# Graph network on one core: SyncE fetches one chunk of edges in some units row by row

## The chip, the cores and the metric

The kernel runs on one core of one Trainium2 chip. The metric is the device time of a run in microseconds (us); of several runs the median is given. The profile is that of one execution, with its own time.

## The reference

Four graph layers follow each other on 12500 nodes of 128 features and 212500 edges, which are sorted by their destination. Each layer adds to `x`: `x = x + layer(relu(layernorm(x)))`. The first is a pair of graph attention convolutions, the second a transformer convolution with a feed-forward part, the third takes a maximum over messages, and the fourth a mean over neighbours. The last two are what this change touches; cut to what matters they are:

```python
# layer 3
msgs = z[dst] @ Wd + z[src] @ Ws + edge_weight[:, None] * ww[None, :] + bm
agg  = segment_max(msgs, dst)
x    = x + relu(z @ W1a + agg @ W1b + b1) @ W2 + b2
# layer 4
h      = relu(layernorm(x))
sums   = segment_sum(h[src], dst)
x      = x + sums / maximum(counts, 1)
```

Each pass over the edges reads one table row for each edge, `table[src[e]]`, and reduces the rows of equal `dst`.

## The kernel before

The nodes are cut into 98 tiles of 128 (T = 98), the edges into 1661 chunks of 128 edges, and the chunks into 98 units of 17 (U = 17). In a unit the chunks are taken in six groups, five of 3 and one of 2 (GS = 3, NG = 6). As edges are sorted by destination, tile t needs the chunks of unit t and a few of its neighbours: 23 windows.

There are five edge passes, one after the other: two for the attention convolutions (`gat`), one for the transformer convolution (`attn`), then the maximum's (`maximum`, table `ts_`, rows of 512 bytes) and the last sum's (`total`, table `th`, rows of 516 bytes). In each, line 1245 fetches the rows of a chunk: one indirect DMA of GpSimd (POOL) for 128 edges, whose row numbers stand in a column of `IDX`. So each pass has 1661 gathers. A group's rows land in a tile `g` of 3 chunks; the maximum's pass has 20 such buffers, the sum's 24.

What follows a gather in the maximum: PE adds the chunk's part of the weights (lines 1711 and 1713, into `pg`), DVE runs a scan over the edges (line 1716), PE transposes (line 1722), ACT copies (line 1726). In the sum nothing stands between the gather and the last matmul. In both, ACT makes or casts a one-hot matrix for each batch of up to four windows (`sef`, line 1291, in the sum from a stored `se`), and PE multiplies the one-hot matrix with the chunk's rows into the tile's sum `acc` (line 1300). A buffer `g` comes free when its last reader has finished.

A tile ends with `ends`: SP loads `gt` (line 1307), ACT copies `acc` (line 1321), and the pass's `post` follows. In the sum that is `after_sum`: DVE divides and adds `x` (line 942 makes `o`), and SP stores `o` to the output (line 944, `out_x` in the trace). SP (SyncE) also loads `x` of the next tile (line 737) and `se` (line 1262) or the features of its edges.

The order is written by hand. `edge_pass` puts generators on a calendar of rounds, 24 rounds for a unit (RU = 24), each with a rank within its round; in every round each live generator takes one step. The gathers of unit u start 24 rounds before the round u x 24, one group every four rounds; the batches of tile t lie in the rounds from t x 24 + 10 (sum) or + 12 (maximum) on. Each engine executes its instructions in the order in which they are written there. A DMA's wait holds up all that stands behind it on the engine that issues it.

Before the first pass, `prepared` sorts out the edge lists: it holds the source numbers of all edges in `sd` (128 partitions, 13 chunks each) and writes them, transposed, to `IDX`.

Of the kernel before, what the change touches and what calls it, by code (L numbers as in the profile page):

```python
# [65 lines left out]
def gnn_kernel(ctx, tc, a, out):  # L66
# [18 lines left out]
    ww_d = dram.tile([3, D], BF16, name="ww_d")  # L85
    feat_d = dram.tile([T, 5, EW], BF16, name="feat_d")
    last_d = dram.tile([T, 5, EW], BF16, name="last_d")
    ewf_d = dram.tile([3, CP * P], BF16, name="ewf_d")
    first_d = dram.tile([1, (CP + 16) * P], BF16, name="first_d")
    xd = dram.tile([NP, D], F32, name="xd")  # L90
# [197 lines left out]
    def chunks(out, x, on):  # L288

        o = out.rearrange("p (r b) -> p r b", b=RC)  # L290
        for b0 in range(0, RC, 4):
            n = min(4, RC - b0)
            px = psum([P, 4, P], "b", "px")
            for b in range(n):
                PE.transpose(px[:, b, :], x[:, (b0 + b) * P:(b0 + b + 1) * P], ident)
            yield
            on(o[:, :, b0:b0 + n].rearrange("p r b -> p b r"), px[:, :n, :])
# [118 lines left out]
    def prepared(wp):  # L416
        tn_i = wp.tile([P, 1], I32, name="tn_i")
        GP.iota(tn_i, pattern=[[0, 1]], base=0, channel_multiplier=P)
        tid = wp.tile([T, 1], I32, name="tid")
        GP.iota(tid, pattern=[[0, 1]], base=0, channel_multiplier=1)  # L420
        tn = wp.tile([P, 1], F32, name="tn")
        V.tensor_copy(tn, tn_i)
        tn1 = wp.tile([P, 1], F32, name="tn1")
        V.tensor_scalar_mul(tn1, tn, -1.0)
        tn2 = wp.tile([P, 1], F32, name="tn2")
        V.tensor_scalar_add(tn2, tn, float(P))
        yield

        w = rd_[:, 1:EW + 1]
        eq = wp.tile([T, EW - P], BF16, name="eq")
        long_ = wp.tile([T, 1], F32, name="long_")
        V.scalar_tensor_tensor(eq, w[:, P:], 0.0, w[:, :EW - P], op0=ALU.add, op1=ALU.is_equal,
                               accum_out=long_)
        yield
        f = wp.tile([T, 2], F32, name="f")
        V.tensor_scalar(f[:, 0:1], rd_[:, 0:1], tn[:T, :], long_, op0=ALU.is_ge, op1=ALU.max)
        V.tensor_scalar(f[:, 1:2], rd_[:, EW + 1:], tn2[:T, :], f[:, 0:1], op0=ALU.is_lt,  # L440
                        op1=ALU.max)
        V.tensor_scalar_min(f[:, 1:2], f[:, 1:2], 1.0)
        yield
        p2 = psum([P, P], "mm", "p2")
        PE.transpose(p2[:1, :T], f[:, 1:2], ident[:T, :T])
        yield
        flag = wp.tile([1, T], F32, name="flag")
        V.tensor_copy(flag, p2[:1, :T])
        zr = wp.tile([1, T], F32, name="zr")
        V.memset(zr, 0.0)  # L450
        ord_ = wp.tile([1, T], F32, name="ord_")
        V.tensor_tensor_scan(ord_, flag, zr, 0.0, op0=ALU.add, op1=ALU.add)
        V.tensor_copy(NOV, ord_[:, T - 1:T])

        at = wp.tile([1, T], F32, name="at")
        V.scalar_tensor_tensor(at, flag, -float(2 * T), ord_, op0=ALU.mult, op1=ALU.add)
        V.tensor_scalar_add(at, at, float(2 * T - 1))
        yield
        pfl = psum([P, P], "mm", "pfl")
        PE.matmul(pfl[:, :T], ones[0:1, :], flag, start=True, stop=True)  # L460
        p3 = psum([P, P], "mm", "p3")
        PE.transpose(p3[:T, 0:1], at, ident[0:1, 0:1])
        yield
        V.tensor_copy(FLAG, pfl[:, :T])
        at_i = wp.tile([T, 1], I32, name="at_i")
        V.tensor_copy(at_i, p3[:T, 0:1])
        GP.indirect_dma_start(out=list_d, in_=tid, in_offset=None,
                              out_offset=bass.IndirectOffsetOnAxis(ap=at_i[:, 0:1], axis=0),
                              bounds_check=T - 1, oob_is_err=False)
        SY.dma_start(LIST, list_d.rearrange("(p t) c -> p (t c)", p=1))  # L470
        yield

        yield from chunks(IDX, sd, V.tensor_copy)

        ch = wp.tile([P, RC * P], F32, name="ch")
        V.tensor_tensor(ch, dd[:, 1:], dd[:, :RC * P], ALU.not_equal)
        yield
        yield from chunks(FIRST, ch, S.copy)
        m = wp.tile([P, RC * P], BF16, name="m")
        S.mul(m, ch, -BIG)  # L480
        SY.dma_start(first_d[0, P:(CP + 1) * P].rearrange("(p f) -> p f", p=P), m)
        yield
        dl = w
        V.tensor_scalar(dl, w, tn1[:T, :], FAR, op0=ALU.add, op1=ALU.min)
        V.tensor_scalar_max(dl, dl, -1.0)
        yield
        xb = wp.tile([T, EW], BF16, name="xb")
        S.copy(xb, dl)
        SY.dma_start(feat_d[:, 2, :], xb)
        hi, lo = yield from square(wp, dl, [T, EW], "q")  # L490
        for k, y in ((3, hi), (4, lo)):
            SY.dma_start(feat_d[:, k, :], y)
        yield
# [707 lines left out]
    def zero_rows(pool):  # L1201
# [3 lines left out]
        for _ in zeroed(gen_d, z, 7):  # L1205
            for _ in range(2 * RU):
                yield

    class Pass:


# [10 lines left out]

        made, whole = True, True

        def __init__(self):
            self.rhs, self.gs, self.f, self.fa, self.x, self.n0 = {}, {}, {}, {}, {}, {}
            self.st, self.se, self.acc = {}, {}, {}

# [6 lines left out]
        def x_load(self, t):  # L1235
            if self.source is not None:
                self.x[t] = features(self.source, t, self.width)
            yield

        def gather(self, u, i):  # L1240
            c, n = groups_of(u)[i]
            g = self.pool.tile([P, GS, self.wid], self.dt, name="g", bufs=self.bufs)
            for j in range(n):
                k = u * U + c + j
                GP.indirect_dma_start(  # L1245
                    out=g[:, j, :], out_offset=None, in_=self.table,
                    in_offset=bass.IndirectOffsetOnAxis(ap=IDX[:, k:k + 1], axis=0))
            self.gs[u, i] = g
            yield
# [81 lines left out]
    def edge_pass(name, table, wid, dt, wids, work_of, post, extra=()):  # L1331
        nonlocal ps_now
        w = work_of
        with tc.tile_pool(name=name, bufs=2) as pool, \
                tc.tile_pool(name="ps_" + name, bufs=1, space=PSUM) as pp, tc.manual_schedule():
            ps_now, w.pool, w.table, w.wid, w.dt, w.wids = (pp, w.banks), pool, table, wid, dt, wids
            cal = {}

            def at(r, rank, g):
                cal.setdefault(r, []).append((rank, g))  # L1340

            for u in range(T):
                r0 = u * RU
                at(r0 - RU, 0, w.load(u))
                at(r0 + RU - 4 - w.tail[0] * (u == T - 1), 0, w.load2(u))
                for i, _ in enumerate(groups_of(u)):
                    at(r0 - RU + i * RG, 0, w.gather(u, i))
                    at(r0 + i * RG, 5, w.e1(u, i))
                    if w.e2_at is not None:
                        e2_at = w.e2_at if u < T - 2 else w.e2_last or w.e2_at  # L1350
                        at(r0 + e2_at[i] - w.tail[0] * (u == T - 1), 4, w.e2(u, i))
                if w.chain_at is not None:
                    at(r0 + w.chain_at - w.tail[0] * (u == T - 1), 3, w.chain(u))
                n = len(w.batches(u))
                rt = r0 + w.tile_at
                loads = rt - RU
                rt -= w.tail[1] * (u == T - 2) + w.tail[2] * (u == T - 1)
                at(min(loads, rt + RU - 9 - 3 * (n - 1) - 2), 0, w.tile_load(u))
                at(rt, 0, w.x_load(u))
                for b in range(n):  # L1360
                    at(rt + RU - 9 - 3 * (n - 1 - b), 2, w.batch(u, b, n))
                at(rt + RU - 4, 1, w.ends(u, post))
            for g in extra:
                at(0, 1, g(pool))
            live, r = [], min(cal)
            while live or cal:
                live += cal.pop(r, [])
                live.sort(key=lambda g: g[0])
                live = [g for g in live if next(g[1], live) is not live]
                r += 1  # L1370
# [116 lines left out]
        V.tensor_tensor(c, x, b, ALU.subtract)  # L1487

    class gat(Pass):
        chain_at, e2_at, tile_at = RU + 5, range(RU + 13, 2 * RU + 1, 2), 2 * RU  # L1490

        def __init__(self, c, source=None):
# [116 lines left out]
            return r  # L1609

    class attn(Pass):
        bufs, source, width = 17, x2d, 2 * D
        chain_at, tile_at = RU + 7, 2 * RU + 2
        e2_at = [RU + 15 + r for r in (0, 2, 4, 6, 7, 11)]
# [68 lines left out]
            return r  # L1683

    class maximum(Pass):
        feats, bufs, source, made = last_d, 20, xd, False
        tile_at, tail = 12, (0, 0, 8)
        banks = {"pm": 1, "x": 2, "acc": 1, "pg": 2, "mm": 2}
# [45 lines left out]
            return r  # L1734

    class total(maximum):
        bufs, made = 24, True
        tile_at, tail = 10, (0, 0, 0)
        banks = {"acc": 2, "mm": 2}
# [173 lines left out]
```

## Time and profile before

| | |
|---|---|
| median of 10 runs | 14941.93 us (14930.65 to 14956.68) |
| the profiled execution | 14932.26 us |
| its span | 14930.6 us |
| maximum's gathers, from and to | 9794 to 12395 us of the span |
| last sum's gathers, from and to | 12484 to 14901 us |
| a gather on POOL | 947 ns |
| POOL, PE, ACT, DVE busy | 53%, 52%, 31%, 31% of the span |

The page gives for each engine its busy time as a share of the span; what an engine waits for, and its register and semaphore instructions, are not counted as busy. The table of windows gives the same for stretches of the span, here the two passes that change. A line such as `L1245 POOL DMA_INDIRECT g<-th,IDX` names the code line, the engine, the operation and what is written from what. In timelines, the bracket behind an instruction says how long its engine sat idle ahead of it, and what ended that. "remote" stands for a releaser that the profile could not name, "issue" for time in which the engine waited for nothing that the profile shows.

### The profile page before, as it was taken

The page shows a single profiled execution, that of the slowest core. Times are in us where ns is not written, and L with a number is a line of the kernel's source. Part 1 is how long each engine was busy: PE and PEld are TensorE (multiplying, and loading weights), DVE is VectorE, ACT ScalarE, POOL GpSimd, SP SyncE. Part 2 cuts the span into 40 slices and gives each one's busy share as a digit, 9 for nine tenths or more (in the row PEclk, how much of TensorE's full clock was granted, in tenths as well). Part 3 has the DMA queues.
Part 4 walks back from the last instruction along what each step waited for, and adds up shares of the span by engine and source line. Part 5 has one row for each costly group of instructions (what it writes and reads, how often), then busy time and mean ns, then how long its engine had stood idle before and what let it go on. Part 6 is the DMA issues. An engine that isn't in the chain of part 4 may idle for free. (4 is left out here: it accounts for less than half of the span.)

```text
span 14930.6 us, 149840 instructions
## 1 busy us (share of the span) xinstructions
PE 7823.4 (52%) x47184; PEld 6072.7 (41%) x47185; DVE 4584.4 (31%) x15188; ACT 4646.7 (31%) x13171; POOL 7876.6 (53%) x8330
## 2 busy tenths in 40 slices
PE   4444444444555555455555555567888774333334
PEld 2222222223444444344444444445666553333333
DVE  4333333332333333344444444423333331000000
ACT  4444444442333333233333333323333332111111
POOL 3455455445555555444444444446555565666666
PEclk5555555555555655677777777777777776666666
DMA  4222122123333333333333333322222222222222
GB/s 112 54 55 49 48 49 49 48 53 81 86 86 86 85 83 86 91 100 97 96 98 101 97 96 98 101 60 79 73 75 75 76 76 59 67 71 68 68 67 69
DMA packets 759391, 1146.93 MB, mean 77 GB/s; under 512 B 224152, under 2 KB 491623, under 8 KB 758479
## 3 DMA queue, kind: packets, MB, share of 16 engines
q0 software_dynamic: 292368, 610.29, 17.3%
q1 hardware_dynamic: 465536, 526.83, 11.2%
q8 instruction: 374, 6.13, 0.2%
q14 instruction: 441, 3.61, 0.1%
q10 hardware_dynamic: 672, 0.07, 0.0%
HBM read 964.76 MB, written 171.69 MB: 76 GB/s over the span
## 5 line engine op out<-in xcount | busy, mean ns | idle before, releaser
L1245 POOL DMA_INDIRECT g<-t,IDX x3322 | 3147.3, 947 | 2940.4 <-issue 1951.4
L1300 PE MATMUL acc<-xf,sef 128*128 128x131 f32 (+2 forms) x13458 | 2743.8, 366 | 1088.0 <-issue 413.7
L1300 PEld LDWEIGHTS acc<-xf,sef 128*128 128x128 f32 x13458 | 2387.8, 263 | 1295.2 <-issue 514.1
L1245 POOL DMA_INDIRECT g<-tkv,IDX x1661 | 1574.5, 948 | 2000.5 <-DVE xf L1675 1483.9
L1245 POOL DMA_INDIRECT g<-ts__84,IDX x1661 | 1571.2, 946 | 1120.9 <-issue 417.7
L1245 POOL DMA_INDIRECT g<-th,IDX x1661 | 1571.7, 946 | 934.0 <-issue 539.2
L1300 PE MATMUL acc<-g,sef 128*128 128x129 f32 x4486 | 884.3, 376 | 1564.1 <-ACT sef L1291 1145.4
L1300 PEld LDWEIGHTS acc<-g,sef 128*128 128x128 f32 x4486 | 818.1, 282 | 1630.3 <-ACT sef L1291 1193.0
L1291 ACT CAST sef<-se 128x512 f32<-128x512 fp8e4 (+1 forms) x1755 | 1030.5, 599 | 1203.4 <-remote 915.1
L1528 PE MATMUL ex<-ADX,st 128*128 128x6 bf16 x4486 | 363.3, 176 | 1214.6 <-ACT st L1134 482.8
L1716 DVE TENSOR_TENSOR_SCAN fm<-n,fm,pg 128x384 f32<-128x384 bf16 (+1 forms) x585 | 567.0, 969 | 1346.1 <-PE pg L1713 602.1
L1315 DVE COPY_PREDICATED r<-FLAG,gt 128x129 f32<-128x129 int32 (+2 forms) x490 | 145.0, 296 | 2570.7 <-ACT r L1321 1792.6
L1528 PEld LDWEIGHTS <-st 128*128 128x128 fp8e4 x4486 | 334.1, 116 | 1434.1 <-issue 755.5
L1651 DVE TENSOR_TENSOR g<-qe,g 128x384 f32<-128x384 f32 x586 | 310.6, 530 | 1609.1 <-remote 1309.9
L1726 ACT COPY xf<-pt_f 128x384 f32<-128x384 f32 x586 | 270.6, 462 | 1270.0 <-PE pt_f L1722 384.1
L1141 PE MATMUL pm_st<-fe,NF 5*128 5x384 bf16 (+2 forms) x877 | 381.6, 458 | 532.2 <-ACT se L1134 430.0
L1646 PE MATMUL qe<-q,st 128*128 128x128 bf16 x6729 | 585.9, 249 | 57.9 <-issue 40.8
L1149 PE MATMUL pm_se<-NF,fa 5*128 5x128 bf16 x4486 | 614.1, 277 | 0.0
L1300 PEld LDWEIGHTS <-se 128*128 128x128 fp8e4 x2243 | 238.4, 130 | 912.3 <-issue 559.0
L1134 ACT ACTIVATE se<-pm_se,ones 128x512 fp8e4<-128x512 f32 (+1 forms) x585 | 391.4, 669 | 696.5 <-remote 458.8
L1300 PE MATMUL acc<-xs,se 128*128 128x201 bf16 x2243 | 483.6, 368 | 196.6 <-ACT se L1134 133.1
L1134 ACT ACTIVATE st<-pm_st,ones 128x384 fp8e4<-128x384 f32 (+2 forms) x877 | 469.6, 536 | 358.6 <-PE pm_st L1141 197.5
(1099 smaller groups left out, 12495.8 us busy)
## 6 DMA issues: line engine op xcount, KB each, us to landing
se<-se_d SPq DMA_DIRECT2D x294, 368.0 KB
st<-st_d SPq DMA_DIRECT2D x196, 368.0 KB
g<-t,IDX POOLq DMA_INDIRECT x3322
n<-first_d SPq DMA_DIRECT2D x97, 544.0 KB
st_d<-st SPq DMA_DIRECT2D x98, 368.0 KB
se_d<-se SPq DMA_DIRECT2D x98, 368.0 KB
g<-tkv,IDX POOLq DMA_INDIRECT x1661
g<-ts__84,IDX POOLq DMA_INDIRECT x1661
```

What stands on the lines that cost most here:

```text
L1134: S.activation(out, pm[:, :out.shape[1], :], AF.Relu, scale=-1.0, bias=ones[:, 0:1], saturate=False)
L1141: PE.matmul(pm[:, :n, :].rearrange("p j e -> p (j e)"), NF, f[:, c * P:(c + n) * P], start=True, stop=True)
L1149: PE.matmul(pm[:, j, :], f[:, (c + j) * P:(c + j + 1) * P], NF, start=True, stop=True)
L1245: GP.indirect_dma_start(out=g[:, j, :], out_offset=None, in_=self.table, in_offset=bass.IndirectOffsetOnAxis(ap=IDX[:, k:k + 1], axis=0))
L1291: S.copy(se, self.se[t][:, at, :])
L1300: PE.matmul(acc[:, :m], se[:, j, :], x[:, i, :], start=(b == 0 and j == 0), stop=(b == n - 1 and j == len(ws) - 1))
L1315: V.copy_predicated(r[:, :w], FLAG[:, t:t + 1].to_broadcast([P, w]), self.gt[:, :w])
L1528: PE.matmul(ex[:, 6 * k:6 * k + 6], st, ADX[:, t, :, :].rearrange("p s v -> p (s v)"), start=(first and c0 == 0), stop=(stop and c0 + n - ...
L1646: PE.matmul(qe[0][:, k - c0, :], st, self.q[t][:, s * D:(s + 1) * D], start=(first and s == 0), stop=(stop and s == 2))
L1651: V.tensor_mul(k, qe[0][:, :n, :], k)
L1716: V.tensor_tensor_scan(fm[:, :m, :].rearrange("p j e -> p (j e)"), self.n0[u][:, cols], pg, self.prev, op0=ALU.add, op1=ALU.max)
L1726: S.copy(ft[:, :m, :D], pt[:, :m, :])
```

## The change

In the preparation the source numbers are also written to a table in device memory, `src_x`, one 4-byte number for each edge. In the maximum's pass, in each sixth unit (u = 5, 11, ..., 95), and in the last sum's, in each fourth (u = 3, 7, ..., 95), POOL no longer gathers the unit's last chunk. SP loads that chunk's 128 source numbers into one partition (`rw`), reads them into registers, sixteen at a time, and starts one DMA for each row, from `table` at the register's row to partition q of a tile of its own, `gx` (two buffers). These rows are spread over 136 rounds in the maximum and 88 rounds in the sum, from 124 (maximum) or 76 (sum) rounds ahead of the unit's first round to 11 rounds behind it, with the load of `rw` four rounds earlier; in each round they come first (rank -1). The group's other chunk is gathered by POOL as before, into the same `gx`. The other three passes have `by_row = None`.

```diff
+    src_x = dram.tile([CP * P, 1], I32, name="src_x")
...
+        ch = wp.tile([P, RC * P], F32, name="ch")
+        V.tensor_copy(ch.bitcast(I32), sd)
+        SY.dma_start(flat(src_x), ch.bitcast(I32))
+        yield
         yield from chunks(IDX, sd, V.tensor_copy)
-        ch = wp.tile([P, RC * P], F32, name="ch")
...
+    RR = 16
+    row_regs = [SY.alloc_register(f"row{i}") for i in range(RR)]
...
+        def row_units(self):
+            if self.by_row is None:
+                return [], 0
+            span = self.by_row * RU - 4
+            return [(u, RU // 2 - span) for u in range(T - 1) if u % self.by_row == self.by_row - 1
+                    and u * RU + RU // 2 - span >= -RU], span
+
+        def fetch_rows(self, u, span):
+            g = self.gx[u] = self.pool.tile([P, 2, self.wid], self.dt, name="gx", bufs=2)
+            rw = self.pool.tile([1, P], I32, name="rw", bufs=2)
+            e0 = (u * U + U - 1) * P
+            SY.dma_start(rw, src_x[e0:e0 + P, :].rearrange("(o f) c -> o (f c)", o=1))
+            for r in range(4):
+                yield
+            q = 0
+            for r in range(span - 4):
+                while q < P and q * (span - 4) < (r + 1) * P:
+                    if q % RR == 0:
+                        SY.load(row_regs, rw[0:1, q:q + RR])
+                    v = SY.snap(row_regs[q % RR], min_val=0, max_val=NP - 1)
+                    SY.dma_start(g[q:q + 1, 1, :], self.table[ds(v, 1), :])
+                    q += 1
+                yield
+
         def gather(self, u, i):
             c, n = groups_of(u)[i]
-            g = self.pool.tile([P, GS, self.wid], self.dt, name="g", bufs=self.bufs)
+            by_row = i == NG - 1 and u in self.gx
+            if by_row:
+                g, n = self.gx.pop(u), n - 1
+            else:
+                g = self.pool.tile([P, GS, self.wid], self.dt, name="g", bufs=self.bufs)
...
+            units, span = w.row_units()
+            for u, r in units:
+                at(u * RU + r, -1, w.fetch_rows(u, span))
...
     class maximum(Pass):
+        by_row = 6
     class total(maximum):
+        by_row = 4
```

More of the change, by code (lines that the diff above doesn't have):

```diff
@@ L1223, in gnn_kernel @@
         made, whole = True, True
+        by_row = None
         def __init__(self):
+            self.gx = {}
             self.rhs, self.gs, self.f, self.fa, self.x, self.n0 = {}, {}, {}, {}, {}, {}
@@ L1489, in gnn_kernel @@
     class gat(Pass):
+        by_row = None
         chain_at, e2_at, tile_at = RU + 5, range(RU + 13, 2 * RU + 1, 2), 2 * RU
@@ L1611, in gnn_kernel @@
     class attn(Pass):
+        by_row = None
         bufs, source, width = 17, x2d, 2 * D
```

## The prediction

> **What bounds the kernel now.** I first read the page's busy shares. POOL is the busiest engine at 53%, next to PE at 52%, so no engine is full over the whole span. The table of windows then splits off the two passes that change.
>
> ```profile
> PE 7823.4 (52%) x47184; PEld 6072.7 (41%) x47185; DVE 4584.4 (31%) x15188; ACT 4646.7 (31%) x13171; POOL 7876.6 (53%) x8330
> core 0: us, PE busy (x) PEld busy (x) DVE busy (x) ACT busy (x) POOL busy (x), PEclk, DMA share, GB/s
> 9794.00:12395.00 2601.00, 2014.99 (x11184) 1511.98 (x11184) 789.69 (x2155) 809.45 (x1874) 1570.21 (x1660) 0.73 0.28 75
> 12484.00:14901.00 2417.00, 864.41 (x4342) 799.40 (x4342) 92.13 (x376) 336.00 (x660) 1570.40 (x1660) 0.60 0.28 68
> ```
>
> The maximum's gathers run for 2601 us and the last sum's for 2417 us, 1661 gathers in each: 26.5 and 24.7 us a unit, 1.566 and 1.455 us a gather. POOL is busy for 60 to 65% of these windows. DMA is at 28%, so bytes bound nothing.
>
> Next, the gather's line in the sum's window: what its engine sat idle for.
>
> ```profile
> L1245 POOL DMA_INDIRECT g<-th,IDX x1660: 942/947/1064, 12483.7 to 14899.8; - x185
>   issue: 538.9, 1480
>   PE acc L1300: 231.2, 66
>   remote: 159.0, 99
> ```
>
> A gather is 0.947 us, and "issue" is 0.30 us between two in a row, so back to back they come every 1.25 us: 21.25 us for a unit's 17. What lies over that pace (2417.3 - 1661 x 1.25 = 341 us, and 2600.9 - 2076 = 525 us in the maximum) is time in which POOL waited for a free gather buffer, which PE's last matmul releases. So POOL isn't late in either pass. In the maximum, the matmul that reads a chunk comes 80 to 92 us after its gather was issued, and that gather had landed after some 2.3 us.
>
> The timeline shows how the consumers lag in the sum.
>
> ```profile
> 12582.31 0.51 ACT L1291 CAST sef<-se 128x384 f32<-128x384 fp8e4 x1 [21.79 <-remote]
> 12603.85 0.94 POOL L1245 DMA_INDIRECT g<-th,IDX  x1 [0.30 <-issue]
> 12619.44 0.27 ACT L1321 COPY r<-acc 128x129 f32<-128x129 f32 x1 [36.62 <-remote]
> 12621.35 0.94 POOL L1245 DMA_INDIRECT g<-th,IDX  x1 [16.56 <-PE acc L1300]
> ```
>
> While gathers run back to back, from 12484 to 12605, ACT's casts wait 21 us and then 36 us for PE's releases, though PE's matmuls of one batch took 2 us. The releases come on steps of 0.70 us, up to 5.6 us apart. POOL runs out of buffers, stops for 16.56 us, and within that stop the releases speed up and the tile ends. So the sum is set by consumers, whose pace depends on whether POOL is gathering. After the last gather the sum's tiles take 6.8, 6.2 and 4.5 us (take 6), the maximum's 20.3, 20.0 and 17.9 (take 20).
>
> **The change, part by part.** It removes 16 gathers from the maximum (units 5 to 95, every sixth) and 24 from the sum (3 to 95, every fourth): 40 of 3322.
>
> Upper bound of the gain, POOL's own pace: at the passes' means 16 x 1.566 + 24 x 1.455 = 60 us. At the bare 1.25 us it is 50 us.
>
> Lower estimate, consumers' pace: let a tile take R us while POOL runs and Q while it stops. Sum: 21.25/R + 3.42/6 = 1, so R = 49 us. One gather less takes 1.25 us out of the running time, in which 1.25/49 of a tile was done, made up in 0.15 us of stop: gain 1.10 us, x24 = 26 us. Maximum: 21.25/R + 5.25/20 = 1, so R = 28.8; 1.25/28.8 x 20 = 0.87, gain 0.38 us, x16 = 6 us. Together 32 us. I take the middle of 32 and 60, near 45 us: the R-and-Q split treats a stop as quiet from its first moment, while the releases in the stop above were only fast after some 10 us, so the worth of a gather lies above 32 us. If nothing is gained, because the stops only lengthen, it is 0.
>
> What SP adds: 40 loads of 512 B, 320 register loads of 16 values each, and 5120 single-row DMAs, beside its 4100 DMAs of now. No row of before shows a one-row DMA with a register offset. The nearest are the preparation's one-partition DMAs.
>
> ```profile
> 31.27 0.21 SPq L403 DMA_DIRECT2D list_d<-none  x1
> 55.32 0.30 SPq L470 DMA_DIRECT2D LIST<-list_d  x1
> 13016.57 0.43 SPq L1307 DMA_DIRECT2D gt<-gen_d  x1
> 13028.26 0.70 SPq L1307 DMA_DIRECT2D gt<-gen_d  x1
> ```
>
> So 0.21 to 0.30 us for the issue. The register instructions (the trace has them, the page counts them as not busy) were 3 to 192 ns, and a load of one register 0.46 to 0.49 us in quiet stretches: for 16 values between 0.46 and 16 x 0.49 = 7.8 us, 0.03 to 0.49 us a row. Clean, a row is therefore 0.24 to 0.98 us; I take 0.40 (0.25 + 0.10 + 0.05), nearest to one-partition DMAs, with a load that costs about twice a single one.
>
> Room: four units of the sum are 98.7 us. SP's own 4 DMAs a unit are 1.6 us, 6.4 us in four, which leaves 92.3/128 = 0.72 us a row. In the maximum, six units are 159 us, less 17 us of SP's own DMAs: 1.1 us a row. At 0.40 both fit and the rows are hidden in SP's time of waiting; SP waits 1784 us for line 942 alone:
>
> ```profile
> SPq L944 <- DVE o L942: 1783.9, 70, 100.2
> ```
>
> That wait is also where the danger is. SP works in order. The rows of unit u are spread over the rounds from 76 before to 11 after its start, ahead of everything else in their round, so between two stores of `out_x` (line 944) stand 34 or 35 rows, and behind each store stand the next tile's x, se and gt. Those four DMAs were issued within 2 us of each other; now 35 rows x 0.40 = 14 us stand among them in by-row stretches. The se loads are a tile ahead and gt is used only at a tile's end, so I cost this at nothing while it stays under a tile's 24.7 us. If that cover is gone it costs what the rival below says. A row also waits for DVE's `o` two tiles back, since the store ahead of it does; the gather had four units of lead, the rows keep about two.
>
> A rule speaks against the whole idea. The Trainium skill ("DMA: Bandwidth & Descriptors", section "Bandwidth") holds that transfers under 64 KB are mostly overhead and should be batched. These rows are 512 B: one gather of 128 rows is 1.25 us of POOL, the same rows are 128 x 0.40 = 51 us of SP. The same page ("Latency and other measured facts") gives a register load a floor of about 600 ns; by it 8 loads cost 4.8 us a unit, as good as nothing here.
>
> The bytes are the same as before. The added table of sources (832 KB, one copy on DVE and one DMA in the preparation) I put at 0 to 3 us: the copy is bounded by DVE rows of some 2 us, and the preparation's end waits for other loads. The first three passes are unchanged.
>
> Sum for the likeliest case: 14932.3 - 45 + 1 = 14888 us for the profiled execution, whose span is 14930.6 with 1.7 us around it. That execution lies 9.7 us under the median of 14941.9, so against the median it is 14898.
>
> **The rivals.**
>
> *SP too late (slower).* Beside running gathers SP's steps, too, fall on 0.70 us: the gt load above took 0.43 us at 13016 and 0.70 at 13028; in the sum 19 of 380 SP DMAs took 0.6 us or more, and 32 of 187 semaphore waits took 0.697. In the preparation a register load with its check took 2.1 us at 143 us, beside gathers. One such step a row is 0.70, just inside the room of 0.72; two, 1.4 us, are outside. That is the deciding point. At 1.4: the 67 gathers of four units keep POOL running 83.8 us; less 6.4 for its own DMAs SP has done 55 rows by then; 73 rows at 0.40 in the quiet need 29 us: 113 instead of 98.7 us, +14 x 24 = +340 us, time 15282. If nothing goes faster in the stop, 128 x 1.4 + 6.4 = 186 us: +2090 us. Against it: 95% of the sum's SP DMAs were at their normal length, and so were 848 of 853 in the maximum. Between the two lies a mild form, some rows late: 0 to +340.
>
> *Nothing gained.* POOL gets ahead anyway, so a gather less only lengthens a stop, and the consumers set the same end: 14942, give or take 15. For it: POOL runs 4.2 to 5.3 units ahead in both passes. Against it: the releases are slow only while gathers run.
>
> *POOL's full pace counts.* Gain 60 us: 14882. It is the upper end of the first case and counted with it.
>
> **How the numbers follow.** The likeliest case 0.47 (gain 32 to 60: 14882 to 14910), nothing gained 0.13, SP late 0.40 (half of that under +170 us). A measurement of this kernel can tell about 0.2%, 30 us, from no change. Faster 0.47, same 0.13, slower 0.40. The range runs from 14875 to 15200: some 0.03 below, and 0.15 above it, the part of the late case that comes near two full steps a row.
>
> **What would show it.** Right: 3282 gathers of the last two passes' 3322; the sum's gather window near 2380 us, the maximum's near 2588; POOL's idle time by "PE acc L1300" hardly longer; row DMAs near 0.25 us, 128 of them done in under 92 us, and PE never waiting for gx. Wrong: row DMAs or their waits of 0.70 us in numbers, PE or ACT waiting on gx or se in the sum, POOL's stops longer than before in the units that have rows, and out_x stores every 28 us instead of 24.7.

## The result and the profile after

The changed kernel takes 15845.6 us (median of 8 runs, 15829.7 to 15861.0) against 14941.9 us before: ratio 1.0604, 95% interval 1.0594 to 1.0613, 904 us slower. The forecast of 14898 us had the sign of the change wrong, and the time lies above the range. The profiled execution has a span of 15840.3 us.

One thing has to be known for the numbers further down: the kernel before took about 14940 us in some series of runs (the first condition) and about 10764 us in others (the second), on one chip both, all kernels of a series met the same one, and so each experiment stands only against the kernel before of its own series.

The difference in span, 909.7 us, splits by the starts of the gathers: 15.3 us are lost before the maximum's first gather, 58.1 in the maximum's gathers (2659.0 against 2600.9), 2.4 between the two passes, 792.5 in the sum's gathers (3209.8 against 2417.3) and 41.3 behind the last gather.

The page's line of busy shares of the changed kernel:

```profile
PE 7661.9 (48%) x47184; PEld 5946.8 (38%) x47185; DVE 4586.0 (29%) x15189; ACT 4648.5 (29%) x13171; POOL 7818.1 (49%) x8290
```

Its two passes in the table of windows, columns as before (length; busy time of PE, PEld, DVE, ACT, POOL; clock, DMA share, GB/s):

```profile
9809.00:12469.00 2660.00, 1959.85 (x11173) 1456.37 (x11174) 788.87 (x2154) 808.44 (x1872) 1551.00 (x1645) 0.75 0.27 74
12559.00:15770.00 3211.00, 755.75 (x4318) 723.49 (x4318) 90.01 (x368) 341.64 (x656) 1544.58 (x1637) 0.60 0.22 51
```

POOL does 24 gathers fewer in the sum and is busy for 48% of it instead of 65%. No other engine took over in busy time. The gather's line in the sum says what POOL waits for:

```profile
L1287 POOL DMA_INDIRECT g<-th,IDX x1613: 938/944/1064, 12559.6 to 15769.4; - x180
  PE acc L1342: 1193.0, 136
  issue: 445.3, 1458
```

Its wait for PE to give buffers back went from 231 to 1193 us. So POOL runs out of buffers sooner; somebody behind it is late. The table of waits in the sum's window names who (three of its lines; engine, line, waited for: us in all, times, longest):

```profile
DVE r L1357 <- DMA gt<-gen_d: 2788.1, 81, 47.2
POOL g L1287 <- PE acc L1342: 1193.0, 136, 17.8
ACT sef L1333 <- DMA se<-se_d: 464.9, 69, 11.7
```

SP's own waits show the other side of it:

```profile
SPq L949 <- DVE o L947: 44.8, 67, 6.7
```

In the kernel before, DVE's step waited for ACT's copy, as the same table has it there:

```profile
DVE r L1315 <- ACT r L1321: 1646.8, 49, 103.3
```

Now it waits for `gt` at the end of most tiles; ACT waits for `se`. SP's wait for DVE's `o`, 1784 us before, is 45 us. SP has become the engine that others wait for. What PE and PEld idled ahead of the instructions that read or write the tile gx ended by a DMA of SP in 29 cases, 832 us in all; the profile puts five of them (146 us) down to gx's own rows and the others to the loads of rw and se. The timeline of SP's queue in one tile of the sum (start, length; a series of row DMAs stands in one line; left out are a row and the loads of x and se behind each store, and five rows behind `gt`):

```profile
13506.00 0.37 SPq L949 DMA_DIRECT2D out_x<-o  x1
13507.87 29.89 SPq L1274 DMA_DIRECT2D gx<-th  x29
13537.81 0.37 SPq L1349 DMA_DIRECT2D gt<-gen_d  x1
13540.81 0.37 SPq L949 DMA_DIRECT2D out_x<-o  x1
```

Between one store of `out_x` and the next `gt` stand 30 rows, and the 29 that come in one piece take 29.9 us. From store to store it is 34.8 us. Where the time goes shows when the intervals from one row DMA to the next are sorted by what POOL does just then (worked out from the trace; a gather run is a series of gathers whose starts lie under 1.3 us apart; other SP work between two rows is included):

```
                            changed kernel, sum    changed kernel, sum
                            first condition        second condition
POOL stopped                1585 rows, mean 0.70    none
run up to 5 us old           740 rows, mean 0.73    76 rows, mean 0.70
run 5 to 15 us old           550 rows, mean 1.84   207 rows, mean 0.52
run over 15 us old           196 rows, mean 3.07  2788 rows, mean 0.66
```

The median of undisturbed rows is 0.42 us: 0.08 from the register operation to the move, 0.06 to the DMA, 0.28 to the next. In the first condition's gather runs the same instructions fall on steps of 0.70 us, six of them for many rows in long runs and up to seven (4.9 us); one row of eight (5.59 us) lies 6 us into a stop of POOL. Of the rows that the next row follows directly, 457 of 475 in runs 5 to 15 us old and all 157 in older ones took over 0.6 us; more than 2 us into a stop of POOL, 48 of 1161 did. At the second condition's means the 746 rows of the last two lines would have taken some 1200 us less (an estimate: 550 x 1.32 + 196 x 2.41), more than the 834 us that the sum lost with its end.

### The profile page after: what moved, and what is told of

Its sections match the earlier page's. It is cut to its first block, busy times and chain, and to the rows that moved or that the text cites. A ratio compares the mean times of both kernels' runs of the same rounds, so it can differ in the third digit from the quotient of the medians.

```text
span 15840.3 us, 165842 instructions
## 1 busy us (share of the span) xinstructions
PE 7661.9 (48%) x47184; PEld 5946.8 (38%) x47185; DVE 4586.0 (29%) x15189; ACT 4648.5 (29%) x13171; POOL 7818.1 (49%) x8290
## 5 line engine op out<-in xcount | busy, mean ns | idle before, releaser
L1342 PE MATMUL acc<-xf,sef 128*128 128x131 f32 (+2 forms) x13458 | 2696.5, 361 | 990.8 <-issue 385.7
L1342 PEld LDWEIGHTS acc<-xf,sef 128*128 128x128 f32 x13458 | 2347.7, 259 | 1195.4 <-issue 493.9
L1287 POOL DMA_INDIRECT g<-th,IDX x1613 | 1522.2, 944 | 1748.3 <-PE acc L1342 1193.0
L1287 POOL DMA_INDIRECT g<-ts__85,IDX x1629 | 1536.7, 943 | 1193.6 <-issue 389.0
L1342 PE MATMUL acc<-g,sef 128*128 128x129 f32 x4294 | 750.0, 351 | 1827.1 <-ACT sef L1333 1761.9
L1342 PEld LDWEIGHTS acc<-g,sef 128*128 128x128 f32 x4294 | 719.0, 263 | 1856.5 <-ACT sef L1333 1792.3
L1363 ACT COPY r<-acc 128x129 f32<-128x129 f32 (+2 forms) x392 | 106.5, 272 | 2276.0 <-remote 1316.3
L1770 PE MATMUL pt_f<-ident,fm 128*128 128x128 f32 x1661 | 390.2, 354 | 500.3 <-DVE xf L1773 341.3
```

The source lines that it names most:

```text
L1287: GP.indirect_dma_start(out=g[:, j, :], out_offset=None, in_=self.table, in_offset=bass.IndirectOffsetOnAxis(ap=IDX[:, k:k + 1], axis=0))
L1342: PE.matmul(acc[:, :m], se[:, j, :], x[:, i, :], start=(b == 0 and j == 0), stop=(b == n - 1 and j == len(ws) - 1))
L1770: PE.transpose(pt[:, j, :], fm[:, j, :], ident)
```

## The experiments

**The parts one by one.** Rows in the maximum alone:

```diff
     class total(maximum):
-        by_row = 4
+        by_row = None
```

> Rows by SP in the maximum's pass alone (16 units); the sum as before. From the profiles, before to after: gathers of the maximum 2601 to 2659 us, the start of the sum's 61 us later counted from the maximum's first, 15 us already lost ahead of the maximum. Theory S (SP's own steps get slow beside back-to-back gathers, so the rows are late in both passes): +60 to +80 us, 15002 to 15022. Rival G (the maximum gains its 6 to 25 us, and what it lost in the changed kernel comes from elsewhere): 14917 to 14937.

Measured: 10875.8 us against 10772.1 (second condition), ratio 1.0091 (1.0074 to 1.0108), +104 us. The expectation's numbers were for the first condition, so only the sign can be read: rows in the maximum cost time. Where, against the next kernel, which has no rows in the maximum and ran in the same series: the gathers took 2114 us instead of 2074, and from the last gather of the maximum to the first of the sum it was 90 us instead of 28. The stores of `th` follow each other every 22.1 us instead of 21.1.

Rows in the sum alone:

```diff
     class maximum(Pass):
-        by_row = 6
+        by_row = None
```

> Rows by SP in the sum alone (24 units). Theory S: SP is the engine that sets the sum; the sum from its first gather to the end goes from 2447 to 3281 us, so with the preparation's share +830 to +850 us, 15770 to 15790, and the SP rows take 0.42 us while POOL stands still and 1.4 us or more while it gathers. Rival M (the sum only lost because the maximum handed it over later): under +100 us.

Measured: 10758.5 us against 10772.1, ratio 0.9985 (0.9976 to 0.9995): 14 us faster. Neither theory had named a gain. It was the first sign that the condition decides: the rows that cost 834 us in the first are hidden in the second. The sum's gathers took 2044 us, 30 us less than the 2074 of the kernel before, which is 24 x 1.25.

Rows in the sum alone that nobody reads, POOL gathering everything:

```diff
-            g = self.gx[u] = self.pool.tile([P, 2, self.wid], self.dt, name="gx", bufs=2)
+            g = self.pool.tile([P, 2, self.wid], self.dt, name="gx", bufs=2)
```

> As the run with rows in the sum alone, but POOL gathers all 1661 chunks as before and nobody reads the rows that SP fetches. Theory S: what costs is SP's time, and the tile's gt, se, x and out_x wait in SP's queue behind the rows whether the rows are read or not: +750 to +1000 us, 15690 to 15940. Rival D (PE waits for the row-fetched chunk itself, as it lands late): with no reader the loss is gone, 14942 to 15000.

Measured: 10786.0 us, ratio 1.0014 (1.0005 to 1.0024), +14 us, as much as the table of sources alone (below). So in the second condition 3072 row DMAs on SP beside POOL's gathers showed no cost of their own, read or not. The question between S and D was put for the first condition and isn't settled by this run. The changed kernel's waits show both there, DVE's for gt (2788 us) and PE's ahead of gx; they overlap, and both are SP's lateness.

What a gather less is worth:

```diff
-            for j in range(n):
+            for j in range(n - (self.made and self.bufs == 24 and i == NG - 1 and n > 1)):
...
-                self.rhs[u * U + c0 + j] = self.gs[u, i], j
+                self.rhs[u * U + c0 + j] = self.gs[u, i], 0 if i == NG - 1 else j
```

> The kernel before, without the last chunk's gather in each of the sum's 98 units (97 of them have a sixth group of two); the matmul reads the chunk ahead of it twice, so all work of PE, ACT, DVE and SP stays. It measures what a gather less is worth, at 97 instead of 24. At POOL's pace (1.455 us each): -141 us, 14801. At the consumers' pace (1.10 us each): -107 us, 14835. If POOL's stops only lengthen: 0, 14942.

> Once more the kernel before without the last chunk's gather in each of the sum's units (97 gathers less; the matmul reads the chunk ahead of it twice). At a POOL pace of 1.25 us it gave -119 us where the kernel before takes about 10770, and should again. Where it takes about 14932, the question is what a gather is worth there: -141 us at the pass's mean, -107 us by my split into running and stopped time, 0 if POOL's stops only lengthen.

Measured, both in the second condition: 10652.8 against 10772.1 (0.9888, 0.9872 to 0.9905) and 10644.5 against 10763.9 (0.9887, 0.9870 to 0.9903): -119 us, 1.23 us for each of 97 gathers. That is POOL's bare period. In the second condition POOL paces the sum; what a gather is worth in the first was not measured.

**The kernels again in the second condition.**

> The changed kernel itself, timed beside the kernel before on the chip of this call. The first four runs were on a chip where the kernel before took 10772 us, and POOL's gathers ran at 1.25 us each all through the last two passes. If the chip of this call is like that: theory P (POOL sets the sum there, SP's rows cost 0.42 us and hide; the maximum's consumers are held up by rows in SP's queue) gives the sum of the parts, +104 for the maximum's rows and -13 for the sum's, with the preparation's 13 us counted once: +78, 10850. Theory S (SP's rows are late in the sum) gives +900. If the chip is like the first one, both give +904.

Measured: 10832.9 us against 10764.2, ratio 1.0074 (1.0057 to 1.0090), +69 us; the sum of the parts was +78. The sum's part of the SP queue, same lines as above:

```profile
9522.74 0.37 SPq L949 DMA_DIRECT2D out_x<-o  x1
9524.61 14.95 SPq L1274 DMA_DIRECT2D gx<-th  x29
9539.61 0.36 SPq L1349 DMA_DIRECT2D gt<-gen_d  x1
9542.74 0.37 SPq L949 DMA_DIRECT2D out_x<-o  x1
```

A piece of 29 rows takes 15.0 us instead of 29.9, beside gathers that never stop. It fits into a tile of some 21 us, and DVE waits for gt 7 times, 132 us in all, instead of 81 times and 2788. What makes the changed kernel slower here is the maximum: of the 50.4 us between its profiled span and that of the kernel before (next run), 61 lie between the last gather of the maximum and the first of the sum, 10 in the maximum's gathers, 10 in the rest, and the sum gives 30 back.

> The kernel before, for its profile on the chip of this call. If it takes about 10772 us: gathers every 1.249 us in the sum, 2074 us for 1661, ACT's casts never waiting 20 us for PE, and SP's DMAs never 0.6 us or longer in the sum. If it takes about 14942 us: as in the profile shown.

Measured: 10766.3 us, and the profile is as expected. The timeline of ACT in the sum:

```profile
9520.22 0.62 ACT L1291 CAST sef<-se 128x512 f32<-128x512 fp8e4 x1 [1.20 <-PE acc L1300]
9521.94 0.62 ACT L1291 CAST sef<-se 128x512 f32<-128x512 fp8e4 x1 [1.10 <-PE acc L1300]
```

The gather's line there:

```profile
L1245 POOL DMA_INDIRECT g<-th,IDX x1661: 940/944/1066, 8682.8 to 10756.5; - x185
  issue: 398.0, 1224
  PE acc L1300: 110.3, 362
  DMA g<-th,IDX: 22.9, 75
```

A gather takes 0.944 us, against 0.947 in the first condition; what is different is that ACT hears of PE after 1.1 us and not after 21. So the 0.70 us steps belong to the first condition and not to POOL's gathers as such.

The table of sources alone:

> Only the table of sources in the preparation; no rows by SP anywhere. My prediction said 0 to 3 us. The profiles say the first gather starts 13 us later (129.3 to 142.6 us): +13 us. Rival: the start is made up in the first pass, 0.

Measured: 10778.8 us, ratio 1.0015 (1.0005 to 1.0025), +14.6 us. The first gather starts at 143.7 us instead of 129.0. In the profile of the changed kernel the store of `first_d` comes at 75.0 us instead of 64.2, and the loads of x behind it move as well. What holds it up is a step of DVE that ran at 47.1 us in the kernel before:

```profile
61.00 1.89 DVE L481 TENSOR_TENSOR ch<-dd 128x1664 f32<-128x1664 f32 x1 [13.76 <-DMA src_x<-ch]
```

The copy of the source numbers is short (1.02 us), but it lies in `ch`, the tile that this step writes next. So the step waits until the DMA to `src_x` has read it, and that DMA was issued at 55.1 us only, behind the other DMAs in SP's queue. The prediction's 0 to 3 us had the copy and not this wait.

**Where the maximum loses.** Rows in the maximum alone, without those in its last units:

```diff
-            return [(u, RU // 2 - span) for u in range(T - 1) if u % self.by_row == self.by_row - 1
+            return [(u, RU // 2 - span) for u in range(T - 1 - 12 * (self.by_row == 6)) if u % self.by_row == self.by_row - 1
```

> Rows in the maximum alone, but only up to unit 83: none in the units 89 and 95, so that none stand in SP's queue in the pass's last 17 units. On a chip where rows in the maximum cost +104 us: theory T (the cost is the lag of the last tiles, seen as 90 instead of 28 us between the last gather of the maximum and the first of the sum) gives +13 (preparation) to +35; theory Q (each tile's chain runs 1 us longer, 22.1 instead of 21.1 us, while rows are being issued, and what is lost early isn't made up) gives 14/16 of 91 us, +13: +80 to +95.

Measured: 10850.4 us against 10764.2, ratio 1.0078 (1.0061 to 1.0095), +86 us: theory Q. The loss builds up tile by tile and isn't only a late end. SP's timeline in the run with rows in the maximum alone, around a store of `xd`, suggests why:

```profile
7907.69 0.35 SPq L742 DMA_DIRECT2D x<-xd  x1
7908.15 0.26 SPq L1307 DMA_DIRECT2D fa<-last_d  x1
7908.60 4.06 SPq L1274 DMA_DIRECT2D gx<-ts__85  x7
7919.74 0.35 SPq L932 DMA_DIRECT2D xd<-x  x1
7920.29 1.48 SPq L1274 DMA_DIRECT2D gx<-ts__85  x4
7921.83 0.88 SPq L1747 DMA_DIRECT2D w<-ewf_d  x3
```

After `7908.60` SP stands for 7 us: the store of `xd` waits for DVE, and the rows behind it wait with it. Then rows come ahead of w, n, gt, x and fa of the tiles that follow. In the kernel before, in the second condition as well, w was issued 0.37 us after that store; here it is 2.1:

```profile
7902.82 0.32 SPq L927 DMA_DIRECT2D xd<-x  x1
7903.19 0.92 SPq L1699 DMA_DIRECT2D w<-ewf_d  x3
```

That this delay is what lengthens the tile by 1 us was read from the timeline, not tried by itself.

Fewer of them, one unit of sixteen, in the maximum alone:

```diff
     class maximum(Pass):
-        by_row = 6
+        by_row = 16
```

> Rows by SP in the maximum alone, in one unit of sixteen (6 units) instead of one of six, so some 8 rows stand in SP's queue for each tile instead of 21. At one of six they cost +89 us besides the table (+104 less 15). Theory Q1 (each tile's chain grows with the rows in SP's queue): 8/21 of it, +34, with the table +49, 10815. Theory Q2 (the chain has about 1 us of room a tile, 20.2 against POOL's 21.2, and only what goes over it counts): the chain's growth stays inside, so only the table is left, less 6 gathers of 1.25 us: +8, 10775. On a chip like the first one I can't say beforehand: +15 to +60.

Measured in the first condition: 14978.1 us against 14931.5, ratio 1.0029 (1.0018 to 1.0040), +47 us, of which some 15 are the table's. That lies in the +15 to +60 given for this condition. It fits Q1's number, too, but that was worked out for the other condition, so it doesn't tell Q1 from Q2.

**Does SP's time decide?** The rows in the sum alone, each fetched twice, in the second condition:

```diff
+            self.gy = self.pool.tile([P, 2, self.wid], self.dt, name="gy", bufs=2)
...
+                    SY.dma_start(self.gy[q:q + 1, 1, :], self.table[ds(v, 1), :])
                     SY.dma_start(g[q:q + 1, 1, :], self.table[ds(v, 1), :])
```

> Rows by SP in the sum alone, and each row is fetched twice (the second copy into a tile that nobody reads), so SP's time per row goes from 0.42 to about 0.76 us (a move and a DMA more) where nothing disturbs it. It asks whether SP's time decides, on a chip where the rows are hidden (-14 us with the table). Theory S: a by-row stretch of four units needs 128 x 0.76 + 8 x 1.23 + 6.4 = 113 us of SP against the 84 us that POOL needs for 67 gathers, so SP sets the pace: 24 x 29 = +700 us on 10758, 11400 to 11500. Rival: SP's rows run beside everything and only their landing counts (lanes, DMA engines at a third of their time): within 30 us of 10758. On a chip like the first one (14942 before): theory S says worse than the +840 of single rows, by 24 x 40 us or more.

Measured: 11813.3 us against 10771.2, ratio 1.0966 (1.0948 to 1.0985), +1042 us. The rows come every 0.84 us (the median, the same in all parts of gather runs) instead of the 0.76 I had estimated; 128 x 0.84 + 9.8 + 6.4 = 124 us of SP a by-row stretch, and 24 x (124 - 84) = 960. Where rows were hidden, doubling SP's time for them brings a loss at least as large as that of the first condition, with the waits that the changed kernel had there:

```profile
DVE r L1359 <- DMA gt<-gen_d: 2830.9, 91, 34.6
ACT sef L1335 <- DMA se<-se_d: 1524.2, 70, 26.9
POOL g L1289 <- PE acc L1344: 1035.0, 222, 16.0
```

**The rows in the sum alone, with the table out of the way.** The copy and the DMA of the table stand at the end of the preparation:

```diff
-        V.tensor_copy(ch.bitcast(I32), sd)
-        SY.dma_start(flat(src_x), ch.bitcast(I32))
-        yield
         yield from chunks(IDX, sd, V.tensor_copy)
...
             SY.dma_start(feat_d[:, k, :], y)
         yield
+        V.tensor_copy(ch.bitcast(I32), sd)
+        SY.dma_start(flat(src_x), ch.bitcast(I32))
+        yield
```

> Rows by SP in the sum alone, and the table of sources is written at the end of the preparation instead of ahead of the IDX and FIRST chunks (same copy, same DMA, no second tile). Two chips so far ran the kernel before in 10764 to 10772 us, and there rows in the sum alone gave -14 us, which I read as -30 (24 gathers of 1.25 us) +15 (the table, measured alone as +14.6). Theory P: with the table out of the way -25 to -30 us, ratio 0.9972 to 0.9977. Rival: the rows themselves cost half of the gain and the table was only a shift; then -14 again, 0.9987. On a chip like the first one (14942): +820 to +850 us.

> Rows by SP in the sum alone with the table of sources written late, again. Where the kernel before takes about 14932 it took 15756, and should again. Where it takes about 10764: 24 gathers of 1.25 us less and no table in the way, -25 to -30 us, about 10736; the rival that the table was only half of the 13 to 15 us gives -14.

Measured: the first time it met the first condition: 15756.0 us against 14931.5, ratio 1.0552 (1.0538 to 1.0567), +825 us, as expected for it; the rows in the sum alone make nine tenths of the change's loss. The second time it met the second condition: 10728.7 against 10761.4, ratio 0.9972 (0.9960 to 0.9983), 33 us faster. There it beats the kernel before and the changed one. The first gather starts at 128.6 and 129.9 us: the table's 15 us are gone.

**Do breaks between gathers relieve SP?** This was to tell whether it is the unbroken run of gathers that slows SP in the first condition. A POOL memset of 0.31 us follows each gather of the sum, without and with SP's rows (late table):

```diff
                     in_offset=bass.IndirectOffsetOnAxis(ap=IDX[:, k:k + 1], axis=0))
+                if self.bufs == 24:
+                    if self.pad is None:
+                        self.pad = self.pool.tile([P, 400], F32, name="pad", bufs=1)
+                    GP.memset(self.pad, 0.0)
```

> The kernel before, with a POOL memset of 128x400 after each of the sum's 1661 gathers, so that they come every 1.7 us or so instead of 1.25 (28.9 us a unit), without any SP rows. Where the kernel before takes about 14932: theory F (back-to-back gathers hold up what the other engines signal, and breaks between them relieve that) says that ACT's casts stop waiting 20 us for PE, and POOL alone sets the sum: 1661 x 1.7 = 2824 us instead of 2417, +400; rival (each gather holds them up by a fixed amount, breaks or not) says the consumers keep their pace and POOL still stops for buffers. Where it takes about 10770: POOL sets the sum anyway, 2824 instead of 2074, +750.

> The kernel with rows by SP in the sum alone and the late table, with the same memset after each POOL gather of the sum. Where the kernel before takes about 14932: theory F says that a row costs SP about 0.42 us nearly everywhere, SP's rows fit (128 x 0.42 + 9.8 + 6.4 = 70 us of the 114 that 67 gathers need), and the sum is POOL's, 1637 x 1.7 = 2783 us: 41 us under the spaced kernel without rows, and 400 us under the same rows without spacing (15756), so about 15300. Rival: rows stay at 1.4 us and more in gather runs, and the sum stays near 3200 us, 15750. Where the kernel before takes about 10770: 41 us under the spaced kernel without rows.

> Rows by SP in the sum alone, with a memset of 0.31 us after each POOL gather of the sum (a gather every 1.56 us). Where the kernel before takes about 10764 it gave 11248, as POOL's pace says, and should again. Where the kernel before takes about 14932: theory F says that the breaks let SP issue a row in about 0.42 us, so the sum is POOL's, 1637 x 1.56 = 2560 us and the kernel about 15080, 670 us under the same rows without breaks (15756). Rival (each gather holds SP up by a fixed amount, breaks or not): the rows stay at 1.4 us and more in gather runs, 15700 to 15800.

> The same rows with a memset of 0.31 us after each POOL gather of the sum. Where the kernel before takes about 10764: 11250 as twice before. Where it takes about 14932: theory F (breaks relieve SP) about 15080; rival (each gather holds SP up by a fixed amount) 15700 to 15800.

> As the run before it. Where the kernel before takes about 14932: theory F (breaks between POOL's gathers relieve SP) about 15080, rival (each gather holds SP up by a fixed amount) 15700 to 15800. Where it takes about 10764: 11250.

Measured: all met the second condition. 11283.9 us without rows against 10763.9 (1.0481, 1.0464 to 1.0499): 1661 x 0.313 us, POOL's pace again (the break is 0.31 us and not 0.45). With rows 11248.5 (1.0450, 1.0433 to 1.0468), and in three later series 11252.1 (1.0456, 1.0426 to 1.0486), 11253.1 (1.0456, 1.0437 to 1.0475) and 11285.8 (1.0461, 1.0405 to 1.0517). So, within the first series, 35 us less with rows, of the 24 x 1.56 = 37 that POOL's pace says. For the first condition the question stays open.

## Why the prediction was wrong

**What bound the kernel.** In the first condition the trace reads as predicted: consumers set the sum, and their releases came on 0.70 us steps; no run tried it there. In the second condition POOL sets it, and the gain is POOL's pace, as the 97 gathers less showed. That the same program has both was not to be seen from one profile.

**The gain, 45 us.** Not reached and, for the first condition, not measured. In the second the 24 gathers of the sum gave 30 us (24 x 1.25), the bare-pace bound; the maximum gave nothing, as its tiles took 1 us longer each with rows.

**The step that failed: SP's 0.40 us a row.** Clean it is 0.42, or 0.50 with its part of the register loads, which the 0.40 had included; both lie inside the room of 0.72. But I took the clean value for the whole pass, and so called the rows hidden in SP's time of waiting. In the first condition only half of the sum's rows were issued while POOL stood still; a quarter were in gather runs older than 5 us and took 1.8 to 3.1 us on the mean. The profile of before had the number: the register load beside gathers at 143 us had taken 2.1 us in steps of 0.70. I argued it away with 95% of SP's DMAs being of normal length. Sorted by gather runs, these DMAs of the sum show what the sample lacked: 180 of 378 were issued in runs 5 to 15 us old, and 12 of these took 0.6 us or more, but only two were issued in runs over 15 us old. They come four at a time when a tile ends, and the one set of four that began in such an old run took 4.15 us from `out_x` to the end of `gt`, where a set in a stop of POOL takes 1.76. So the sample nearly left out the stretch in which rows got slowest, and it said little on a queue that is busy all the time. Why the sets in runs 5 to 15 us old came through in 1.96 us, while the rows there were slow, isn't shown.

Two readings of that part were off as well. The load of sixteen values, 1.23 us, is two and a half single ones and not two, so the eight of a unit are 9.8 us and not 4.8. And of the 32 semaphore waits put at 0.697 us sixteen were that long; all lay between 0.64 and 0.71.

**The late rival.** Its mechanism is what happened: SP's steps too long beside gathers, gt and se late, `out_x` behind them, and a deciding time for a row: in the second condition 0.42 us was hidden and 0.84 was not. Its price was too small. I let SP do 55 rows at 1.4 us while POOL runs and the rest at 0.40 in one quiet stretch: 113 us for four units. Measured: 3209.8/98 x 4 = 131. The 196 rows in runs over 15 us old took 3.1 us each, and the quiet rows 0.70 with the other SP work among them. The extra was 32 us a by-row stretch instead of 14, and it left my range.

**Cover for gt, se and x.** I costed the rows among the four DMAs of a tile at nothing "while it stays under a tile's 24.7 us". 29.9 us for the rows of one tile went over it: DVE waited for gt at 81 tile ends, and the stores of `out_x` came every 32.3 us on the mean, where 28 was my sign of being wrong. "PE never waiting for gx", a sign for being right, failed as well.

**The table.** +13 to +15 us instead of 0 to 3, as DVE's next step had to wait for the DMA that read its tile.

**Pass by pass.** The maximum was forecast at 2588 us of gathers and took 2659; as the timeline reads, rows that stand behind a blocked store and ahead of the next loads lengthen each tile.

What stays open: what makes the first condition. Its 0.70 us steps are in the traces on SP and on PE's releases. On SP they stand beside gathers and in the first 2 us behind them, seldom later, and the delays grow with the age of a gather run. Gathers are not slower in it, and neither are the DMA engines: the packets of POOL's queue took 17.3% of the kernel before's 14931 us in it and 25.1% of 10765 us in the second. In the sum the clock granted to TensorE was no lower in it, 0.60 against 0.56. Whether breaks between gathers would relieve it was not seen.

## What to carry to other kernels

A queue that mostly waits isn't spare time: work put into it stands behind its waits and ahead of its next loads, so count, for each load behind it, the time of what is now in front, at the slowest rate that the profile shows for that engine and not at the clean one. Give the moved work a deciding rate (here 0.72 us a row), and look in the trace for any stretch in which that engine was both busy and disturbed; samples that miss the longest such stretches don't bound it. A table that only a late stage needs belongs at the end of a preparation that is one chain, and where it is written from a tile, ask which step writes that tile next.

## What the runs showed of the hardware

The same program took 14932 us and 10764 us on one chip in two series of runs, with gathers of the same 0.944 to 0.947 us; what differed is how soon other engines' steps came through beside gathers (a row DMA with its two register steps: 0.42 us, or up to 4.9). A single-row DMA of SP with a register offset costs 0.42 us of the sequencer (0.228 for the DMA, 0.044 for the register operation, 0.029 for the move, and the gaps), and 1.23 us for a load of sixteen registers. 0.42 us for one row stands against 1.25 us of POOL for 128.
